# Six broadcast loads per graph, issued by ScalarE instead of SyncE

## The chip, the cores and the metric

The kernel runs on one core of a Trainium2 chip. The metric is the time of one execution on the device in microseconds (us), and a kernel's time is the median of its runs. Engines are called by the names of the profile: PE is TensorE (matrix products; PEld is its weight load), DVE is VectorE, ACT is ScalarE, POOL is GpSimd and SP is SyncE. SPq stands for the instructions that SP's sequencer runs, among them those that issue DMAs.

## The reference, cut to what matters

There are 64 graphs of 256 nodes with 512 features each (x is 64 x 256 x 512), an adjacency matrix of 0 and 1 (64 x 256 x 256), and four layers of the form x = x + layer(relu(layernorm(x))). Layers 0 and 3 weight the rows of a product by a softmax over the nodes, layer 2 is an attention with tanh, and layer 1, in which the change lies, is an attention of 8 heads with one score per node and head for the node itself and one for it as a neighbour:

```python
feats = einsum('bnf,hfu->bhnu', X, W)
e_self = einsum('bhnu,hu->bhn', feats, a_self)
e_neigh = einsum('bhnu,hu->bhn', feats, a_neigh)
dense = leaky_relu(e_self[..., :, None] + e_neigh[..., None, :], 0.2)
dense = dense + NEG_BIG * (1.0 - A[:, None])
out = einsum('bhij,bhju->bhiu', softmax(dense, axis=-1), feats) + b
x = x + relu(out)            # after the heads are put side by side
```

## The kernel before, in words

**Tiles.** All is in float32. A graph's 256 nodes lie on 128 partitions, two to a partition (NC = 2), so that x of one graph is a tile of 128 x 1024 ("xt"). Twenty-three such tiles are the "big" buffers, thirteen of 128 x 512 are the "mid" ones, and eight PSUM tiles the "bank" ones. A step takes a buffer by `Graph.take` (L739) and the last user gives it back with `done` (L748); the next taker in the plan gets it, so a tile's first writer waits for the last reader of what lay there before.

**Order.** Each graph is cut into 209 named steps (`graph`, L1020). No scheduler decides their order: every step has a planned time, written out by hand. `TIMES` (L41) holds them for most graphs; `FIRST` (L85) has own tables for the first nine and `LAST` (L398) for the last eight; graph b's times are moved by b x 52.8 (`PERIOD`, L40). `Plan.sequence` (L703) sorts all steps of all graphs by time, and `Plan.run` (L711) calls them in that order and ties each instruction to the one before it on the same engine. So each of PE, ACT, DVE, POOL and SP runs its instructions in exactly the order of the plan, and the planned times themselves have no other effect. A graph's steps spread over more than 300 us of the plan, so steps of several graphs lie between each other on each engine. Where a step's instruction must wait, all that the plan has after it on that engine waits too. SP issues all DMAs of the kernel before.

**The attention of layer 1.** Its scores lie with the nodes on the partitions (tile `ec`, steps `ec0`, `ec1`), and are needed twice as rows as well, the same row on all 128 partitions. That goes by way of DRAM:

- `send` (L1378): DVE transposes `ec` into `er`.
- `er` (L1382): SP writes `er` to DRAM as `er_d`, in four DMAs (L1386).
- `en0`, `en1` and `es0`, `es1` (`spread`, L1388, with its DMA at L1393): four loads, each of four heads' rows of `er_d`, repeated over 128 partitions: a big tile of 512 KB. The n tiles hold the scores that belong to L1407, the s tiles those that belong to L1445. `en0` and `es1` stand close behind `er` in the plan, `en1` and `es0` later.
- `max0` to `max3` (`largest`, L1399): DVE finds the largest masked score of each row from an n tile and the mask in PSUM (L1407). `mxv`, `mxt` (L1418 to L1430) put it into rows, and `mr` (L1430) has SP write it to DRAM as `m_d`, in four DMAs (L1434).
- `mb0`, `mb1` (`spread` again, L1393): two loads of `m_d`, broadcast in the same way.
- `ea` (L1445, ACT, reads an s tile), `eg` (L1452, POOL, adds the mask), `eb` (L1458, DVE, subtracts the maxima in an m tile), `ex` (L1464, ACT, exp), then `po` (L1476, PE) and `eh` (L1487, POOL), for each of four pairs of heads.

So six loads per graph, 384 in all, go through L1393.

**What lies around them in the plan, of other graphs.** Norms: the squares of a row on ACT (`sx`, L1082), then `rs` (L1088, ACT), the power -0.5 (L1092, POOL), the shift (L1097 and L1098, POOL), and the normed rows (`hn`, L1103, ACT). DVE transposes these (`sq`, L1012), SP writes them to DRAM as `sq_d` (L1123) and gathers them in another order (L1017, L1286; four DMAs each). Sums: `yp` (L1675, ACT) makes one half of a layer's output, and `ya` (L1063, DVE) adds it to x and takes the row sums. ACT also has `om` (L1536, the attention's rows divided by their sums), `am` (L1688, the adjacency by the mask), the copy `va` (L1210), the exponentials of a softmax over nodes (`softa`, L1141 and L1143), its scale (L1152), `aw3` (L1716) and the tanh of layer 2 (`ta`, L1664). DVE's L1202 and L1333 are sums of products; L1657 multiplies by the mask. PE's products are L1188 and L1476 among others.

Of the kernel before, what the change touches and what calls it, by code (L numbers as in the profile page):

```python
# [726 lines left out]
class Graph:  # L727
# [5 lines left out]
    def step(self, name):  # L733
        def add(run):
            self.steps[name] = run
            return run
        return add
# [21 lines left out]
def tile_four_gnn_layers(ctx: ExitStack, tc: tile.TileContext, x, adj, nodemask,  # L759
# [6 lines left out]
    nc = tc.nc  # L766
# [253 lines left out]
    def graph(b):  # L1020

        g = Graph(plan)
# [365 lines left out]
        def spread(name, kind, src, users):  # L1388
            for q in range(2):
                def halves(q=q):  # L1390
                    @step(f"{name}{q}")
                    def _():
                        nc.sync.dma_start(g.take("all", users, name=f"{kind}{q}"),  # L1393
                                          src()[q * HA:(q + 1) * HA].partition_broadcast(P))
                halves()
        spread("en", "n", lambda: st["er_d"][H:], 2)
# [365 lines left out]
```

## Time and profile before

| what | value |
|---|---|
| runs of the kernel before | 3695.48, 3696.07 and 3696.09 us, median 3696.07 |
| the profiled execution's own time | 3695.02 us |
| its span | 3693.2 us |
| PE clock that was granted, mean | 0.981 of full speed |
| instructions | 61,427 |
| DMA: one queue | 70.3% of 16 engines' span, 781 MB |
| idle ahead of DVE's L1012, mostly for ACT's L1103 | 143.6 us |
| idle ahead of DVE's L1407, for er_d loads | 4.1 us |
| idle ahead of DVE's L1458, for m_d loads | 6.5 us |
| idle ahead of ACT's L1445, for er_d loads | 3.1 us |

The profile is of one execution. Its span runs from the first to the last instruction seen, and the 1.8 us by which the execution's own time is longer lie around it. Busy times are sums over an engine's instructions and do not count register, semaphore and DMA-issuing instructions. In a line of a timeline the columns are the start (us from the start of the span), the length (us), the engine, the line of the kernel, the operation, what it writes and reads by the program's names with partitions x elements and type, and how many like it follow each other; an idle time before it stands behind, in brackets, with the instruction that ended it. A line of the waits gives the waiting instruction, the one that it waited for, and the total idle time, how often, and the longest. Who ended a wait is inferred from semaphore events.

### The profile page before, as it was taken

Reading aid. Unit: us, or ns where it says so; the run is one execution under the profiler, and the core shown is the slowest. Engines: PE = TensorE matmul, PEld = TensorE weight load, DVE = VectorE, ACT = ScalarE, POOL = GpSimd, SP = SyncE. Lnnn points to the kernel's source line nnn. Section 1 sums busy time; section 2 is a strip of 40 time slices with the busy share of each in tenths; the row PEclk is TensorE's granted clock in tenths of the full one; section 3 lists DMA queues with packets and bytes.
Section 4 is the critical chain, followed back from the end, with each engine's and each line's share of the span. In section 5 each row is a group of like instructions: output and inputs, shape, how many; then the busy total and the mean of one; then the engine's idle time right before and its main releaser. Section 6 shows DMA issues by size and latency. Waiting matters only on the chain.

```text
span 3693.2 us, 61427 instructions
## 1 busy us (share of the span) xinstructions
PE 3401.5 (92%) x16834; PEld 2175.5 (59%) x16834; DVE 3314.2 (90%) x8248; ACT 2781.7 (75%) x6533; POOL 2270.6 (61%) x2452
## 2 busy tenths in 40 slices
PE   5688999999999999999999999999999999989988
PEld 3455655665665666666666666666666666556554
DVE  6789998999999999999999989999989999999985
ACT  3667777787787787787778778778878778778765
POOL 3565665666666666666666666666666666565653
PEclk8799999999999999999999999999999999999999
DMA  6666766777777777777777777777777777767663
GB/s 185 181 188 208 207 213 212 222 220 216 222 219 218 222 222 217 225 224 224 227 215 221 226 216 217 230 222 219 226 216 219 223 219 221 217 204 216 197 190 119
DMA packets 995143, 785.28 MB, mean 213 GB/s; under 512 B 791984, under 2 KB 862192, under 8 KB 994800
## 3 DMA queue, kind: packets, MB, share of 16 engines
q1 hardware_dynamic: 994800, 781.35, 70.3%
q8 instruction: 137, 2.24, 0.2%
q14 instruction: 206, 1.69, 0.1%
HBM read 511.12 MB, written 270.01 MB: 212 GB/s over the span
## 4 chain that ended last, share of the span: by engine, by line
POOL 22%; DVE 18%; issue 15%; PE 14%; DMA 12%; ACT 7%; SPq 6%; POOLq 0%; ACTq 0%; DVEq 0%
PE bank L1188 9%; DMA big<-sq_d 8%; SPq L1017 5%; DVE big L1458 4%; DVE junk L1407 3%; POOL big L1452 3%; POOL rstd L1092 3%; POOL mid L1487 3%; POOL big L1173 3%; DMA sq_d<-big 3%; POOL big L1172 2%; POOL big L1179 2%; DVE big L1202 2%; DVE big L1012 2%; ACT big L1082 2%
## 5 line engine op out<-in xcount | busy, mean ns | idle before, releaser
L1188 PE MATMUL bank<-t_s,big 128*128 128x264 f32 (+3 forms) x3072 | 978.0, 452 | 8.3 <-DVE big L1657 6.1
L1188 PE MATMUL bank<-w_s,big 128*128 128x264 f32 (+2 forms) x3072 | 850.9, 410 | 45.9 <-DMA big<-sq_d 36.3
L1188 PEld LDWEIGHTS bank<-t_s,big 128*128 128x128 f32 x3072 | 583.0, 194 | 306.5 <-issue 180.5
L1188 PEld LDWEIGHTS bank<-w_s,big 128*128 128x128 f32 x3072 | 583.8, 196 | 278.5 <-issue 131.8
L1452 POOL TENSOR_TENSOR big<-big,mid 128x1024 f32<-128x1024 f32 x256 | 604.0, 2370 | 98.6 <-ACT big L1445 89.0
L1012 DVE STREAM_TRANSPOSE big<-big 128x512 f32<-128x512 f32 x640 | 483.6, 782 | 143.6 <-ACT big L1103 143.5
L1092 POOL TENSOR_TENSOR rstd<-rstd,power 128x2 f32<-128x2 f32 x256 | 183.9, 718 | 678.8 <-ACT rstd L1088 628.2
L1103 ACT ACTIVATE big<-big,shift,rstd 128x512 f32<-128x512 f32 x512 | 387.7, 805 | 167.3 <-POOL shift L1098 167.0
L1172 POOL TENSOR_TENSOR big<-big 128x256 f32<-128x256 f32 x256 | 226.6, 885 | 412.9 <-DMA big<-sq_d 278.7
L1487 POOL TENSOR_TENSOR mid<-big 128x512 f32<-128x512 f32 x256 | 377.1, 1493 | 138.2 <-ACT big L1464 138.2
L1407 DVE CUSTOM_DVE_ANT_0 junk<-big,bank 128x256 f32<-128x256 f32 x1024 | 428.9, 419 | 35.3 <-DMA big<-er_d 4.1
L1082 ACT ACTIVATE big<-big,sum 128x512 f32<-128x512 f32 x512 | 363.8, 712 | 116.7 <-DVE sum L1333 83.7
L1445 ACT ACTIVATE big<-big,ec 128x256 f32<-128x256 f32 x1024 | 428.8, 496 | 5.4 <-DMA big<-er_d 3.1
L1202 DVE TENSOR_TENSOR big<-bank,big 128x320 f32<-128x320 f32 (+1 forms) x704 | 399.5, 571 | 18.2 <-PE bank L1188 13.7
L1476 PE MATMUL bank<-big,big 128*64 128x256 f32 x2048 | 260.7, 388 | 92.2 <-ACT big L1464 91.9
L1458 DVE TENSOR_TENSOR big<-big,big 128x1024 f32<-128x1024 f32 x256 | 325.2, 1309 | 6.5 <-DMA big<-m_d 6.5
L1633 PE MATMUL bank<-big,big 64*128 64x256 f32 x2048 | 283.8, 398 | 50.5 <-DVE mx L1407 31.4
L1657 DVE TENSOR_TENSOR big<-bank,mid 128x512 f32<-128x512 f32 x512 | 319.9, 677 | 5.3 <-PE bank L1633 5.2
L1664 ACT ACTIVATE big<-big 128x512 f32<-128x512 f32 x512 | 293.1, 619 | 14.3 <-DVE big L1657 12.3
L1464 ACT ACTIVATE big<-big 128x1024 f32<-128x1024 f32 x256 | 267.8, 1052 | 41.4 <-DVE big L1458 33.6
L1633 PEld LDWEIGHTS bank<-big,big 64*128 64x128 f32 x2048 | 219.7, 197 | 131.4 <-ACT big L1621 65.1
L1536 ACT ACTIVATE big<-big,rs 128x64 f32<-128x64 f32 x1024 | 257.4, 334 | 24.5 <-DVE rs L1525 13.2
(132 smaller groups left out, 5877.8 us busy)
## 6 DMA issues: line engine op xcount, KB each, us to landing
sq_d<-big SPq DMA_DIRECT2D x448, 512.0 KB
big<-sq_d SPq DMA_DIRECT2D x1792, 128.0 KB
big<-er_d SPq DMA_DIRECT2D x256, 512.0 KB
big<-m_d SPq DMA_DIRECT2D x128, 512.0 KB
big<-in_x_dram SPq DMA_DIRECT2D x64, 512.0 KB
out_dram<-big SPq DMA_DIRECT2D x64, 512.0 KB
mid<-in_adj_dram SPq DMA_DIRECT2D x64, 256.0 KB
mid<-in_adj_dram SPq DMA_DIRECT2D x256, 64.0 KB
```

The source lines that it names most:

```text
L1012: nc.vector.transpose(sq.rearrange("p (r k i c) -> p c k r i", r=4, k=KC, c=NC)[:, c], t[:, c])
L1082: nc.scalar.activation(g["hn"][:, c, :], g["xt"][:, c, :], AF.Square, scale=-float(D), bias=st["sum"][:, c:c + 1], accum_out=st["ssq"][:, ...
L1103: nc.scalar.activation(g["hn"][:, c, :], g["xt"][:, c, :], AF.Relu, bias=st["shift"][:, c:c + 1], scale=st["rstd"][:, c:c + 1])
L1188: nc.tensor.matmul(p, a()[:, k], w[:, k], start=(k == 0), stop=(k == 1))
L1202: nc.vector.tensor_tensor(out(), g[i][:, :w], old(), OP.add)
L1407: nc.vector.tensor_tensor_reduce(junk, g[f"n{h // HA}"][:, h % HA, :], g["far"][:, c * N:(c + 1) * N], 1.0, -BIG, OP.add, OP.max, g["mx"][ ...
L1445: nc.scalar.activation(e[:, s, j, :], g[f"s{h // HA}"][:, h % HA, :], AF.Prelu, bias=st["ec"][:, j, H + h:H + h + 1], alpha=0.2)
L1452: nc.gpsimd.tensor_tensor(e, e, g["negt"][:, None].to_broadcast([P, 2, NC, N]), OP.add)
L1458: nc.vector.tensor_tensor(e, e, g[f"m{p // 2}"][:, p % 2 * 2:p % 2 * 2 + 2, None, :].to_broadcast([P, 2, NC, N]), OP.subtract)
L1487: nc.gpsimd.tensor_tensor(g.take("half", name=f"h{p}"), e[:, :, 0, :], e[:, :, 1, :], OP.add)
L1633: nc.tensor.matmul(ps[s][:, m, :], chunk(g["xpt"][half, p], m), g["xc"][half, p, :], start=True, stop=True)
L1657: nc.vector.tensor_tensor(th[:, s], g[f"ps{p}{s}"].rearrange("p (m n) -> p m n", m=NC), g["at"], OP.mult)
```

## The change

One line of `spread` has another engine issue the DMA. The step's place in the plan, its tiles, the transfer and its source are the same; `Plan.run` ties it to ACT's instruction before it in the plan instead of to SP's.

```diff
@@ -1390,7 +1390,7 @@
                 def halves(q=q):
                     @step(f"{name}{q}")
                     def _():
-                        nc.sync.dma_start(g.take("all", users, name=f"{kind}{q}"),
+                        nc.scalar.dma_start(g.take("all", users, name=f"{kind}{q}"),
                                           src()[q * HA:(q + 1) * HA].partition_broadcast(P))
                 halves()
```

The writes of `er_d` and `m_d` (L1386, L1434), the gathers and all other DMAs stay with SP.

## The prediction

> **What bounds the kernel now.** I read the page's first section, then the waits by engine over the stretch from 734 to 3044 us, in which 43 graphs (12 to 54) run with one and the same order on ScalarE, then the timelines of one of them (graph 32).
>
> ```profile
> PE 3401.5 (92%) x16834; PEld 2175.5 (59%) x16834; DVE 3314.2 (90%) x8248; ACT 2781.7 (75%) x6533; POOL 2270.6 (61%) x2452
> ```
>
> PE and DVE are both near full, ACT has a quarter free. Which of the two binds is seen from who waits: the waits of DVE in that stretch are few (columns: total us, times, longest).
>
> ```profile
> DVE big L1012 <- ACT big L1103: 101.2, 81, 1.5
> DVE bank L1368 <- PE bank L1188: 17.0, 41, 0.4
> DVE big L1270 <- PE bank L1476: 12.7, 42, 1.9
> DVE junk L1407 <- DMA big<-er_d: 1.5, 3, 0.8
> ```
>
> With three smaller ones they are 138 us of 2310: DVE works or steps between instructions for 94% of it, and waits for the six loads 1.5 us in all. So DVE sets the pace, 2310/42 = 55.0 us a graph, and its longest wait is for ACT, by way of ACT, POOL, ACT (a norm). A new wait of DVE is therefore new time, unless an old wait shrinks by as much.
>
> ACT's waits in the same stretch:
>
> ```profile
> ACT big L1082 <- DVE sum L1333: 54.6, 42, 2.5
> ACT big L1082 <- DVE big L1063: 20.0, 41, 1.2
> ```
>
> These two are the slack that I use below: 54.6/43 = 1.27 us and 20.0/43 = 0.47 us a graph. Now the place where the loads go in. SyncE, then ACT, then DVE of graph 32:
>
> ```profile
> 1834.19 1.88 SPq L1386 DMA_DIRECT2D er_d<-er  x4
> 1836.18 2.54 SPq L1017 DMA_DIRECT2D big<-sq_d  x4
> 1839.22 1.30 SPq L1393 DMA_DIRECT2D big<-er_d  x3
> 1843.78 0.32 SPq L1123 DMA_DIRECT2D sq_d<-big  x1
> ```
>
> ```profile
> 1833.41 2.01 ACT L1536 ACTIVATE big<-big,rs 128x64 f32<-128x64 f32 x8
> 1835.33 0.89 ACT L1688 ACTIVATE mid<-mid,mask_c 128x256 f32<-128x256 f32 x2
> 1836.13 0.71 ACT L1082 ACTIVATE big<-big,sum 128x512 f32<-128x512 f32 x1
> ...
> 1837.66 0.72 ACT L1082 ACTIVATE big<-big,sum 128x512 f32<-128x512 f32 x1 [0.73 <-DVE big L1063]
> ...
> 1839.01 1.15 ACT L1675 ACTIVATE big<-big 128x512 f32<-128x512 f32 x2
> 1840.16 1.52 ACT L1103 ACTIVATE big<-big,shift,rstd 128x512 f32<-128x512 f32 x2
> ```
>
> ```profile
> 1839.48 0.69 DVE L1202 TENSOR_TENSOR big<-bank,big 128x512 f32<-128x512 f32 x1
> 1840.08 0.68 DVE L1063 SCALAR_TENSOR_TENSOR big<-big,big 128x512 f32<-128x512 f32 x1
> ```
>
> The reader is to see that er_d is written at 1834.19, that SyncE reads it at 1839.22 only because four gathers stand between, and that ACT is busy right through that time; DVE's L1063 at 1840.08 adds what the first L1675 has written by 1839.64. L1202 just ahead of it has no idle time after it: DVE does not wait here.
>
> **What the Trainium skill says.** "DMA: Bandwidth & Descriptors", section Issuing engines are not separate DMA queues: all issuers feed the same 16 DMA engines, and a second issuer saves only the first one's issue time. All traffic of the trace is on one queue from SyncE, whose issue of such a load takes 426 ns in the median (319 to 1356). The same page, section Anatomy of one DMA: a DMA's semaphore wait is done by the issuing sequencer ahead of the dispatch. The trace agrees: SyncE stood at L1393 for m_d 11.1 us in 19 waits. "Perfetto Trace Analysis", section DVE / Act Engine Instruction: the sequencer pushes compute instructions into a queue where they wait, and goes on. The trace agrees: a semaphore instruction of L1082 ran at 1834.62, ahead of two L1536 and two L1688 that started at 1834.86 to 1835.73, four instructions in front. So an issue with its waits met can hide under queued work; one whose wait is not met stops the sequencer, and the engine runs dry. Same page, section DMA Instruction — HWDGE: an issue locks the descriptor generator, which two sequencers share. No run here shows that yet; it goes into the upper bound.
>
> **The change part by part.** The instruction order of the changed program has 384 DMA issues less on SyncE and 384 more on ACT; the orders of PE, DVE and POOL are the same. In the 43 graphs the places on ACT are: two loads of er_d after the last L1536 and before L1688; a third between L1688 and L1082; the fourth between L1716 and L1103; both loads of m_d between L1143 and L1664.
>
> (1) SyncE loses six issues, 6 x 0.43 = 2.6 us a graph. Worth 0: after the three loads SyncE stood idle from 1840.52 until DVE released L1123 at 1843.78, and after the other ones likewise.
>
> (2) First two er_d loads. They need er_d in memory. The trace's semaphore events tell when each transfer has landed (16 events each): the four er_d writes of graph 32 landed at 1836.84, 1837.15, 1837.33 and 1837.51. ACT is there at 1835.33, so it stops for 2.18 us. Over the 43 graphs the last landing lies 1.90 us after the start of L1688 (1.20 to 3.04). Then come two issues, on SyncE 0.35 and 0.42 us with 0.06 between, some 0.1 for the semaphore instructions ahead and 0.1 to fill the engine again: 1.1 us (estimate from those rows). L1688 is late by 1.90 + 1.1 = 3.0 us. Behind it queue L1688, L1082, L1088, L1210, L1675 and L1103; DVE waits for L1210, L1675 and L1103, POOL for L1088, PE for L1688.
>
> (3) What hides it: the gap of 0.47 us ahead of the second L1082, leaving 2.53; DVE reaches L1063 0.44 us after L1675's half is done (1840.08 against 1839.64; 0.43 to 0.44 in 42 of the 43 graphs), leaving **2.1 us that DVE waits**. The next meeting, L1012 for L1103, had 1.46 us in hand (in three graphs 0.16) and adds nothing. L1141 then waits for DVE, so both are late alike. 43 x 2.1 = **90 us**. DVE's other waits do not shrink: the norms behind them start at a DVE sum (L1333), so they move along.
>
> (4) Third er_d load: 0.38 + 0.05 us under two L1688 of 0.89: 0. Its PE and POOL waits are met by then. Fourth: its data are long there; 0.4 us under the two L1716 (1.3 us): 0, bound 0 to 0.45. It is issued some 3.5 us later than before and lands 5.5 us after, still ahead of L1445, which reads it at 1853.12 before the change and later after.
>
> (5) The m_d loads: m_d lands 0.83 us before L1664 starts in 38 of the 43 (in four 0.1 to 1.5 us after); with 0.97 us for two issues L1664 comes 0.15 to 0.5 us late, and the 1.27 us wait for the sum L1333 after it takes that up: 0. Without that cover 43 x 0.3 = 13 us.
>
> (6) The other 21 graphs, at start and end, have other orders. By the same comparison of landing with ACT's place, er_d stops ACT in graphs 0, 1, 55, 56, 57 (2.8, 2.5, 2.2, 2.9, 2.4 us), m_d in 2, 56, 61 and 63 (6.3, 7.1, 2.1, 7.5 us): 35.8 us. DVE is less full there, so I take half, 18 us (0 to 36), and 5 us for plain issues.
>
> (7) Two queues share the DMA engines in turn. Gathers issued just behind the m_d loads landed after 4.2 us (1861.33 to 1863.25 in graph 32) against 2.7 to 3.0 elsewhere and can gain 1.5; the m_d loads lose up to that and have 1.2 us in hand before L1458. Who waits for those gathers is POOL and PE, not DVE: 0, bounds -0.8 to +0.5 us a graph (-0.8 is all of DVE's waits for PE, 33.0 us over 43).
>
> Sum: 90 + 18 + 5 = 113. The profiled execution took 3695.02 us (span 3693.2), 1 us under the median of 3696.07, so it can stand for it: 3695 + 113 = **3808 us**, 3.1% slower.
>
> **Rivals.** *Absorbed:* the sequencer's four queued instructions, or a faster er_d landing, cover the stop. For it speaks that ACT is idle a quarter of the time; against it that the queue (some 1.2 us) is drained before 1837.5. Needs L1688 under 0.47 + 0.44 = 0.91 us late; gives 3696. *Faster:* the freed gathers, priced at all of DVE's waits for PE: 0.77 x 64 = 49 us, 3646. It decides only below that same 0.91 us, and DVE's waits for PE are mostly behind matmuls whose data were there. *Worse:* each of ACT's issues also waits for SyncE's four gathers, which hold the generator 0.5 to 0.6 us each from 1836.18 to 1838.72: two times 0.6 more, 3.3 x 43 = 142, edges 45: 3882. That the change doesn't do what it says is ruled out by the order.
>
> **How the numbers follow.** This kernel's runs tell a difference above about 0.2% from none. Forecast 0.74, worse 0.14, absorbed 0.06, faster 0.06. Forecast's own range: a DVE wait of 1.2 to 2.7 us a graph (1.90 + x - 0.91, with x, the issues and what lies around them, 0.2 to 1.7 instead of 1.1) and 0 to 41 us of edges, so 3747 to 3852. With most of the worse case it becomes 3745 to 3880, which leaves out the absorbed and the faster case, 0.12 together, and what lies above. Faster 0.06, same 0.06, slower 0.88.
>
> **What would show it.** After: ACT's L1688 idle before it for some 3 us a graph, ended by er_d; DVE's L1063 with a new wait for ACT's L1675 of 2 us a graph; DVE's busy time unchanged; ACT's L1664 hardly late. Wrong if L1063 doesn't wait, if ACT's issues take another length than SyncE's, or if the m_d loads make L1458 wait.

## The result, and the profile after

The changed kernel (called after, as the kernel before is called before) takes 3876.98 us in the median of 4 runs (3871.23 to 3880.58), the kernel before 3695.78 us (3692.90 to 3696.09): a ratio of 1.0491, interval 1.0473 to 1.0509, 181 us more. The profiled execution of after has a span of 3869.5 us, against 3693.2; its own time, 3871.23 us, is 6 us under the median.

The page of after, first section. Busy times are those of before within 1.1%; what falls is the share of the span.

```profile
PE 3436.4 (89%) x16834; PEld 2183.7 (56%) x16834; DVE 3335.0 (86%) x8248; ACT 2782.3 (72%) x6533; POOL 2280.3 (59%) x2452
```

The waits of DVE while graphs 12 to 54 run (767 to 3182 us of after; total us, times, longest). Two lines are new beside the list of before: L1063 waits for ACT's L1675, 76.2/42 = 1.8 us a graph, and L1325 waits for ACT's L1152, 15.4/42 = 0.4 us. L1012 is as it was.

```profile
DVE big L1012 <- ACT big L1103: 102.5, 82, 1.3
DVE big L1063 <- ACT big L1675: 76.2, 42, 3.6
DVE bank L1368 <- PE bank L1188: 17.4, 42, 0.4
DVE big L1325 <- ACT w L1152: 15.4, 42, 2.0
```

ACT's waits in the same stretch. L1688, which never waited before, now does in all 42 cases; the profile files 26 of them under the er_d writes and 16 under "issue", and both are the same stop. The line of L1664 is the place of the two m_d loads.

```profile
ACT mid L1688 <- DMA er_d<-er: 74.4, 26, 4.3
ACT mid L1688 <- issue: 43.3, 16, 3.9
ACT big L1082 <- DVE sum L1333: 39.3, 42, 0.9
...
ACT big L1664 <- DVE tot L1148: 23.9, 40, 1.0
```

Graph 32 in after: SyncE's queue, then ACT, then DVE (start, length, instruction, idle before).

```profile
1914.65 1.76 SPq L1386 DMA_DIRECT2D er_d<-er  x4
1916.51 2.54 SPq L1017 DMA_DIRECT2D big<-sq_d  x4
```

```profile
1913.75 2.02 ACT L1536 ACTIVATE big<-big,rs 128x64 f32<-128x64 f32 x8
1917.59 0.87 ACTq L1393 DMA_DIRECT2D big<-er_d  x2
1918.50 0.51 ACT L1688 ACTIVATE mid<-mid,mask_c 128x256 f32<-128x256 f32 x1 [2.73 <-issue]
1918.61 0.52 ACTq L1393 DMA_DIRECT2D big<-er_d  x1
...
1921.36 1.15 ACT L1675 ACTIVATE big<-big 128x512 f32<-128x512 f32 x2
```

```profile
1919.39 0.68 DVE L1202 TENSOR_TENSOR big<-bank,big 128x512 f32<-128x512 f32 x1
1922.02 0.72 DVE L1063 SCALAR_TENSOR_TENSOR big<-big,big 128x512 f32<-128x512 f32 x1 [1.95 <-ACT big L1675]
```

L1536 ends at 1915.77. The last er_d write landed at 1917.49 (semaphore events of the trace), the first load is issued 0.10 us later, and L1688 starts at 1918.50, 2.73 us after ACT ran dry. DVE is through with L1202 at 1920.07 and stands still for 1.95 us. The third load, at 1918.61, lies beside L1688 and costs nothing. This is the chain that the prediction drew, in the places that it named.

The other new wait, in the same graph. ACT ends L1143 at 1940.75, issues the two m_d loads at 1942.23, and L1664 and L1152 behind them come late for DVE:

```profile
1942.23 0.81 ACTq L1393 DMA_DIRECT2D big<-m_d  x2
1943.09 1.15 ACT L1664 ACTIVATE big<-big 128x512 f32<-128x512 f32 x2 [2.34 <-DVE big L1657]
1944.14 0.28 ACT L1152 ACTIVATE w<-w,tot 128x2 f32<-128x2 f32 x1
```

```profile
1944.46 0.42 DVE L1325 SCALAR_TENSOR_TENSOR big<-big,w,big 128x192 f32<-128x192 f32 x1 [2.05 <-ACT w L1152]
```

The bracket behind L1664 names DVE's L1657. That is not what it waited for: m_d had landed at 1942.21 and the load went out 0.02 us later. Where a DMA issue stands between two instructions of an engine, the bracket can name whatever else came last. (Graph 32 is one of the long cases; in 35 of the 43 ACT stands idle here for 0.56 to 0.58 us, the two issues alone.)

**Where the 176 us are.** I cut both traces at the L1688 of graphs 12 and 54: the start is longer by 32.6 us (734.7 to 767.3), the middle by 105.5 (2309.3 to 2414.8), the end by 38.1. The middle is 76.2 + 15.4 of the two waits, and 11.4 by which four small instructions of DVE have grown (last section); the other 2.5 are the balance of small differences of both signs.

### The profile page after: what moved, and what is told of

It is laid out like the page before. It is cut to its first block, busy times and chain, and to the rows that moved or that the text cites. A ratio compares the mean times of both kernels' runs of the same rounds, so it can differ in the third digit from the quotient of the medians.

```text
span 3869.5 us, 61063 instructions
## 1 busy us (share of the span) xinstructions
PE 3436.4 (89%) x16834; PEld 2183.7 (56%) x16834; DVE 3335.0 (86%) x8248; ACT 2782.3 (72%) x6533; POOL 2280.3 (59%) x2452
## 4 chain that ended last, share of the span: by engine, by line
POOL 21%; DVE 21%; issue 15%; PE 14%; ACT 12%; DMA 11%; SPq 6%; ACTq 0%; POOLq 0%; DVEq 0%
PE bank L1188 9%; DMA big<-sq_d 6%; DVE junk L1407 5%; DVE big L1458 4%; SPq L1017 4%; ACT big L1103 3%; ACT big L1082 3%; POOL rstd L1092 3%; DVE big L1012 3%; POOL big L1173 3%; POOL big L1172 3%; POOL mid L1487 2%; POOL big L1179 2%; DVE big L1202 2%; POOL big L1452 2%
## 5 line engine op out<-in xcount | busy, mean ns | idle before, releaser
L1188 PE MATMUL bank<-w_s,big 128*128 128x264 f32 (+2 forms) x3072 | 852.1, 411 | 46.6 <-DMA sq_d<-big 19.2
L1452 POOL TENSOR_TENSOR big<-big,mid 128x1024 f32<-128x1024 f32 x256 | 603.6, 2368 | 112.9 <-ACT big L1445 105.5
L1012 DVE STREAM_TRANSPOSE big<-big 128x512 f32<-128x512 f32 x640 | 483.3, 781 | 145.7 <-ACT big L1103 145.5
L1103 ACT ACTIVATE big<-big,shift,rstd 128x512 f32<-128x512 f32 x512 | 387.7, 805 | 178.4 <-POOL shift L1098 176.9
L1407 DVE CUSTOM_DVE_ANT_0 junk<-big,bank 128x256 f32<-128x256 f32 x1024 | 428.8, 419 | 52.4 <-DMA big<-er_d 20.5
L1172 POOL TENSOR_TENSOR big<-big 128x256 f32<-128x256 f32 x256 | 226.2, 883 | 404.9 <-DMA big<-sq_d 256.8
L1445 ACT ACTIVATE big<-big,ec 128x256 f32<-128x256 f32 x1024 | 428.8, 496 | 31.0 <-DMA big<-er_d 22.4
L1202 DVE TENSOR_TENSOR big<-bank,big 128x320 f32<-128x320 f32 (+1 forms) x704 | 398.6, 569 | 20.3 <-PE bank L1188 14.5
L1657 DVE TENSOR_TENSOR big<-bank,mid 128x512 f32<-128x512 f32 x512 | 320.4, 677 | 19.4 <-PE bank L1633 15.0
L1458 DVE TENSOR_TENSOR big<-big,big 128x1024 f32<-128x1024 f32 x256 | 326.9, 1315 | 10.8 <-DMA big<-m_d 6.3
L1664 ACT ACTIVATE big<-big 128x512 f32<-128x512 f32 x512 | 290.6, 616 | 51.5 <-DVE tot L1148 25.0
L1063 DVE SCALAR_TENSOR_TENSOR big<-big,big 128x512 f32<-128x512 f32 x256 | 205.9, 819 | 97.2 <-ACT big L1675 89.1
```

Of the source, the lines that this page charges most:

```text
L1012: nc.vector.transpose(sq.rearrange("p (r k i c) -> p c k r i", r=4, k=KC, c=NC)[:, c], t[:, c])
L1103: nc.scalar.activation(g["hn"][:, c, :], g["xt"][:, c, :], AF.Relu, bias=st["shift"][:, c:c + 1], scale=st["rstd"][:, c:c + 1])
L1172: nc.gpsimd.tensor_tensor(m[:, 0], rows_of(1, 0), rows_of(1, 1), OP.add)
L1188: nc.tensor.matmul(p, a()[:, k], w[:, k], start=(k == 0), stop=(k == 1))
L1202: nc.vector.tensor_tensor(out(), g[i][:, :w], old(), OP.add)
L1407: nc.vector.tensor_tensor_reduce(junk, g[f"n{h // HA}"][:, h % HA, :], g["far"][:, c * N:(c + 1) * N], 1.0, -BIG, OP.add, OP.max, g["mx"][ ...
```

## The experiments

The theory after the result: ACT's sequencer takes its instructions in order, so a load placed there stops all later work of ACT until its data are in DRAM, and is itself late where ACT's work ahead of it is late; the cost is that of the place. The rivals: two queues cost as such (issue time, the descriptor generator, transfers that get in each other's way), or the ends of the program pay only for the late middle.

The edits of 1 to 5, 10 and 11 have the same form: a condition that chooses the queue in `spread`. This table cuts each trace as above (us over the kernel before, from one profiled execution each; "all" is the difference of spans):

| kernel | start | middle | end | all |
|---|---|---|---|---|
| after | 32.6 | 105.5 | 38.1 | 176.3 |
| 1 six loads, graphs 12 to 54 | 2.4 | 107.4 | 2.8 | 112.6 |
| 2 six loads, the other graphs | 25.5 | -2.8 | 38.7 | 61.4 |
| 3 en0, es1 | 16.0 | 85.5 | 23.8 | 125.3 |
| 4 mb0, mb1 | 7.7 | 16.8 | 13.5 | 38.0 |
| 5 en1, es0 | 4.9 | 29.7 | 12.0 | 46.6 |
| 6 six loads, er_d replaced by old rows | 31.5 | 41.7 | 45.0 | 118.2 |
| 7 ACT delayed by seven instructions, no load moved | 4.9 | 89.2 | 3.4 | 97.5 |
| 8 ACT delayed by two | 3.5 | 1.3 | 0.9 | 5.7 |
| 9 six loads at later places, graphs 12 to 54 | -1.3 | 15.6 | 3.1 | 17.4 |
| 10 en0, en1, the other graphs | 12.8 | -0.5 | 23.8 | 36.1 |
| 11 es0, es1, the other graphs | 7.3 | -1.3 | 10.7 | 16.7 |
| 12 as 9, m_d loads later still | -0.1 | 0.6 | 2.9 | 3.4 |

**1 and 2, the middle and the ends apart.**

```diff
-                        nc.sync.dma_start(...)
+                        queue = nc.scalar if 12 <= b <= 54 else nc.sync
+                        queue.dma_start(...)
```

```diff
+                        queue = nc.scalar if b < 12 or b > 54 else nc.sync
```

> The six loads on ACT in graphs 12 to 54 only; the other 21 graphs as before. Theory (ACT stops for er_d, DVE is late at L1063, and ACT's stop for m_d makes DVE late at L1325): the 106 us that the trace after shows over these graphs, so 3696 + 106 = 3802 us. Rival (the loss is one of the whole program, two queues hurting each other's transfers): a share of 43/64 of 181, 3818 us, with landing times of the gathers longer everywhere.

> The six loads on ACT in graphs 0 to 11 and 55 to 63 only. Theory: the start and the end cost 29 and 41 us on their own, so 3696 + 70 = 3766 us. As the prediction had it: 3696 + 18 + 5 = 3719 us. Rival (the late middle pushes into the end, so that the end costs less without it): between the two, about 3740 us.

Measured: 3807.82 us, ratio 1.0295 (1.0279 to 1.0310), and 3759.27 us, ratio 1.0168 (1.0151 to 1.0186), both against 3697.30. The first is nearer to the theory's 3802 than to the 3818 of a loss spread over the whole program. 110.5 + 62.0 = 172.5 of 181: the two parts add up within 9 us, and the middle of the second is not slower. The ends have a cost of their own, nearly three times the 23 us of the prediction.

**3, 4 and 5, which loads.**

```diff
+                        queue = nc.scalar if (name, q) in (("en", 0), ("es", 1)) else nc.sync
```

```diff
+                        queue = nc.scalar if name == "mb" else nc.sync
```

```diff
+                        queue = nc.scalar if (name, q) in (("en", 1), ("es", 0)) else nc.sync
```

> Only the first two er_d loads of every graph (en0, es1) on ACT, the other four on SyncE. Theory: L1063 waits as after, 1.8 us a graph with what starts behind it, 82 us in the middle and some half of the 70 us of the ends: 3696 + 82 + 30 = 3808 us; no wait of L1325 for L1152 in the middle. Rival (the loss comes from all six issues, 6 x 0.4 us of ACT a graph): a third of it, 3756 us.

> Only the two m_d loads of every graph (mb0, mb1) on ACT. Theory: L1325 waits for L1152 by 0.3 us a graph as after, 14 us in the middle, and the m_d stops of the ends (graphs 2, 56, 61, 63) 20 us: 3696 + 34 = 3730 us. As the prediction had it: 0 in the middle and some 11 us at the ends, 3707 us.

> Only the third and fourth er_d load of every graph (en1, es0) on ACT. Theory: their data are in memory when ACT gets there, and issues hide under the work that is queued: 0 in the middle; at the ends loads that are issued behind ACT's own work come late, 0 to 15 us: 3696 to 3711 us. Rival (each issue costs ACT its 0.4 us): 64 x 0.8 = 51 us, 3747 us.

Measured: 3822.42 us (1.0339, 1.0324 to 1.0355) and 3736.14 us (1.0111, 1.0094 to 1.0128) against 3697.30; 3743.26 us (1.0115, 1.0100 to 1.0130) against 3698.90. DVE's waits of 3, then of 4 (735 to 3140 us); in 3 the line of L1325 is gone, in 4 that of L1063:

```profile
DVE big L1063 <- ACT big L1676: 72.1, 42, 4.0
```

```profile
DVE big L1325 <- ACT w L1152: 15.2, 43, 1.7
```

(The edit moves later lines by one: L1676 is L1675.) So the er_d loads make the one wait and the m_d loads the other. The three parts sum to 208 us, more than the whole. 5 missed my expectation by 30 us and came near the rival's 3747, but not because each issue costs ACT its time; ACT of graph 32 in 5 tells why:

```profile
1857.13 0.89 ACT L1689 ACTIVATE mid<-mid,mask_c 128x256 f32<-128x256 f32 x2
1859.22 0.33 ACTq L1394 DMA_DIRECT2D big<-er_d  x1
1859.65 0.72 ACT L1082 ACTIVATE big<-big,sum 128x512 f32<-128x512 f32 x1 [1.62 <-POOL big L1179]
```

With the first two loads back on SyncE, the third is the first on ACT to need er_d. That landed at 1859.12, so ACT stops there, two L1688 later than in after (1.52 us in the mean of the 43 graphs), and DVE waits 23.4 us at L1063 in the middle. In after this load is free only because the first had already waited; the parts share one wait and cannot be summed. The bracket again names something else.

**6, the wait taken away.** The loads read rows that were written once at the start.

```diff
+    old = ctx.enter_context(tc.tile_pool(name="old_d", bufs=1, space=DRAM)).tile([E, N], F32, name="old_d")
...
+                if name == "b1":
+                    nc.sync.dma_start(old, t[:E, :N])
...
-        spread("en", "n", lambda: st["er_d"][H:], 2)
+        spread("en", "n", lambda: old[H:], 2)
-        spread("es", "s", lambda: st["er_d"][:H], 2)
+        spread("es", "s", lambda: old[:H], 2)
```

> As after, but the four er_d loads of every graph take their rows from a block in DRAM that is written once at the start (the attention of layer 1 so gets constant scores); er_d is still written. All issues are there, the wait for er_d is not. Theory (the wait is what counts): L1688 at most 0.9 us late, no wait of L1063 in the middle; what stays is L1325's 14 us and the stops for m_d at the ends, so 3696 + 35 = 3731 us. Rival (the issues count): L1688 1.0 us late or more for two issues under a drained queue and the wait of L1063 about 1 us a graph, 3731 + 43 = 3774 us or more.

Measured: 3812.67 us against 3698.90, ratio 1.0299 (1.0282 to 1.0316): far from 3731, and within the rival's "3774 us or more". But the rival's way is not what happened. In the middle L1688 never waits, all three issues lie under L1536 (graph 23, L1539 here), and the eight L1536 ahead of L1688 take 1.93 us, before 1.92:

```profile
1379.01 0.35 ACTq L1396 DMA_DIRECT2D big<-old_d  x1
1379.11 0.58 ACT L1539 ACTIVATE big<-big,rs 128x64 f32<-128x64 f32 x2
1379.46 0.39 ACTq L1396 DMA_DIRECT2D big<-old_d  x1
1379.60 1.05 ACT L1539 ACTIVATE big<-big,rs 128x64 f32<-128x64 f32 x4
1380.39 0.33 ACTq L1396 DMA_DIRECT2D big<-old_d  x1
```

That settles that an issue with its data there costs ACT nothing while work is queued. But the kernel changed more than I meant. DVE still waits 14.0 us at L1063 (L1066 here), in nine graphs; the longest case is this one:

```profile
1389.41 0.69 DVE L1066 SCALAR_TENSOR_TENSOR big<-big,big 128x512 f32<-128x512 f32 x1 [3.94 <-ACT big L1678]
```

L1675 (L1678 here) needed four gathers of L1286, which SyncE had issued from 1377.45 to 1380.03. The last landed at 1388.64, 8.6 us after its issue, and L1675 started 0.11 us later. In the nine cases the last gather took 5.8 to 8.6 us; before the change no gather of L1286 in the middle took more than 4.5. The three loads, which no longer wait for er_d, are in flight beside the gathers: from 1379 to 1385 us the packets of ACT's queue take 63% of the time of the 16 DMA engines and those of SyncE's 22%, where SyncE's had taken 75% in the 2 us before. So a load from one queue can hold up the other queue's transfers, if it starts beside them. The er_d writes come late as well: 4.7 us from issue to landing in the median of the middle, against 2.2 before the change. Part of them are also issued late: the program gives the DMAs of all queues eight completion semaphores in turn (the counters that tell of a landing; 455 or 456 DMAs each before the change), and a DMA waits for the landing of the one eight before it. The third er_d write of graph 23 was issued at 1384.12, 0.01 us after the landing of a load from ACT. So this run is good for L1688 and not for the total. Its ends cost 76.5 us, after has 70.7; but as the slow transfers are in them too, this run doesn't tell what the stop for er_d costs there.

**7 and 8, the delay without the loads.**

```diff
         @step("am")
         def _():
+            for _ in range(7 if 9 <= b <= 51 else 0):
+                nc.scalar.activation(idle_s, idle_s, AF.Copy)
```

(`idle_s` is a tile of 128x256 of its own; in 8 the 7 is a 2. The `am` of graph b stands at the er_d loads of graph b + 3.)

> The kernel before, with seven added ACT instructions of 128x256 (some 0.41 us each, 2.9 us) ahead of L1688 in the middle graphs, and no load moved. Theory (a late ACT at this place is all there is to the er_d part; 0.91 us of it are free): L1063 waits 2.0 us a graph, 43 x 2.0 = 86 us, 3782 us. Rival (two queues matter): no more than ACT's busy time asks, under 40 us.

> The same with two added instructions, 0.82 us. Theory: under the 0.91 us that are free, so within 0.2% of 3696 us and no wait at L1063. Rival (every delay of ACT here is DVE's): 43 x 0.82 = 35 us, 3731 us.

Measured: 3790.61 us, ratio 1.0240 (1.0225 to 1.0255), and 3706.33 us, ratio 1.0020 (1.0011 to 1.0028), against 3698.90. DVE's waits of 7 (L1065 and L1677 are L1063 and L1675):

```profile
DVE big L1014 <- ACT big L1105: 105.6, 84, 1.3
DVE big L1065 <- ACT big L1677: 82.2, 42, 2.6
```

In 7 the added work makes L1688 3.0 us late, and DVE waits 82.2/42 = 2.0 us; in 8 it is 0.76 us late, and L1063 waits 0.8 us over the whole middle, though 8 as a whole is 0.1 to 0.3% slower, at the edge of what can be told. So some 1.0 us is free, near the 0.91 us that the prediction read from two gaps, and a late ACT alone makes the er_d part of the change, without any DMA.

**9 and 12, other places.** The buffers are taken where they were; the issue is a step of its own, with a later time.

```diff
+    "en0_now": 22.500, "es1_now": 22.510, "en1_now": 22.520, "es0_now": 29.000, "mb1_now": 39.360, "mb0_now": 39.370,
...
-                        nc.sync.dma_start(g.take("all", users, name=f"{kind}{q}"),
-                                          src()[q * HA:(q + 1) * HA].partition_broadcast(P))
+                        st[f"{name}{q}"] = g.take("all", users, name=f"{kind}{q}")
+                        if not 12 <= b <= 54:
+                            load(nc.sync)
+
+                    @step(f"{name}{q}_now")
+                    def _():
+                        if 12 <= b <= 54:
+                            load(nc.scalar)
```

In 12 only the last two times differ, 39.500 and 39.510.

> All six loads on ACT in graphs 12 to 54, with buffers taken at the same place, but issued later in ACT's order: the first three er_d loads behind the two L1675 instead of ahead of L1688, the m_d loads behind the first two L1664 and ahead of L1152; the other 21 graphs on SyncE. Theory (it is the place, not the engine): er_d has landed by then, L1063 doesn't wait, L1152 is 0 to 0.3 us late: within 0.3% of the kernel before, 3690 to 3707 us. Rival (two queues cost as such, or ACT pays each issue): 43 x 6 x 0.4 = 103 us at most, 3740 to 3800 us.

> As with the later places, and the m_d loads one step later still: behind L1152, so that DVE's L1325 no longer stands behind them, ahead of the next two L1664. Theory: no wait of L1325 for L1152 (8.6 us less) and none at L1063; the m_d tiles come some 1 us later, which L1458 has in hand: 3715 - 9 = 3706 us, the remainder over the kernel before being DVE's small L1420 to L1427. Rival (loads on ACT cost what they cost wherever they stand): no gain over the later places, 3715 us.

Measured: 9 takes 3714.73 us against 3695.37 (1.0055, 1.0038 to 1.0071), a little more than I had expected. In the middle 9.6 us of it are L1325 waiting for L1152, ahead of which the m_d loads still stand, and 5.8 are the four small instructions of DVE. 12 takes 3695.46 us against 3695.54, ratio 1.0002 (0.9991 to 1.0013), 10 us better than expected: the small instructions too are back within 2.5 us of before. ACT of 12 in graph 32, at the er_d loads (L1685 is L1675), and the head of DVE's waits in its middle, which is the list of before again (L1013 is L1012, L1104 is L1103, and so on):

```profile
1839.51 0.33 ACTq L1404 DMA_DIRECT2D big<-er_d  x1
1839.58 0.63 ACT L1685 ACTIVATE big<-big 128x512 f32<-128x512 f32 x1
1839.86 0.54 ACTq L1404 DMA_DIRECT2D big<-er_d  x1
1840.12 0.62 ACT L1685 ACTIVATE big<-big 128x512 f32<-128x512 f32 x1
1840.44 0.44 ACTq L1404 DMA_DIRECT2D big<-er_d  x1
1840.93 1.52 ACT L1104 ACTIVATE big<-big,shift,rstd 128x512 f32<-128x512 f32 x2 [0.20 <-POOL shift L1099]
```

```profile
DVE big L1013 <- ACT big L1104: 106.4, 87, 1.5
DVE bank L1369 <- PE bank L1189: 17.8, 43, 0.4
DVE big L1271 <- PE bank L1486: 10.9, 43, 1.5
```

258 loads on ACT, at no cost that can be measured, and at no gain: within 0.13%, SyncE's issue time was worth nothing, as step (1) of the prediction had it. No version here beats the kernel before.

**10 and 11, the ends.**

```diff
+                        queue = nc.scalar if name == "en" and not 12 <= b <= 54 else nc.sync
```

```diff
+                        queue = nc.scalar if name == "es" and not 12 <= b <= 54 else nc.sync
```

> Only the loads of the n tiles (en0, en1), and only in graphs 0 to 11 and 55 to 63, on ACT. Theory (at the ends it is mostly the loads that stand behind ACT's work and come late for L1407): L1407 loses 15 to 20 us as after, with ACT's stops for er_d in graphs 0, 1, 2, 10, 11 and 54 to 57 some 30 us, 3728 us. Rival (at the ends too ACT's stops for er_d and m_d are all there is): no loss at L1407, 10 to 15 us, 3710 us.

> Only the loads of the s tiles (es0, es1), and only in graphs 0 to 11 and 55 to 63, on ACT. Theory: no loss at L1407, since the n tiles come from SyncE; L1445 on ACT waits for late s tiles by up to 20 us, of which DVE pays a part: 5 to 20 us, 3703 to 3718 us. Rival: as much as with the n tiles, some 30 us.

Measured, against 3695.37: 3734.39 us (1.0103, 1.0085 to 1.0120) and 3715.36 us (1.0056, 1.0036 to 1.0075). L1407 waited 4.1 us for er_d loads before the change, over the whole run; in after, then in 10 (where L1408 is L1407), it waits:

```profile
DVE junk L1407 <- DMA big<-er_d: 20.5, 10, 4.2
```

```profile
DVE junk L1408 <- DMA big<-er_d: 28.3, 9, 6.5
```

What happens there is seen in after, graph 3. ACT, then DVE:

```profile
235.23 0.30 ACT L1088 ACTIVATE rstd<-ssq,eps 128x2 f32<-128x2 f32 x1
235.37 0.33 ACTq L1393 DMA_DIRECT2D big<-er_d  x1
236.89 0.81 ACT L1103 ACTIVATE big<-big,shift,rstd 128x512 f32<-128x512 f32 x1 [1.37 <-POOL shift L1098]
236.91 0.33 ACTq L1393 DMA_DIRECT2D big<-er_d  x1
```

```profile
239.01 0.42 DVE L1407 CUSTOM_DVE_ANT_0 junk<-big,bank 128x256 f32<-128x256 f32 x1 [3.06 <-DMA big<-er_d]
```

er_d had landed at 230.86; the first load left 4.5 us later, because ACT's own work stood ahead of it, and DVE waited 3.06 us. In nine of the ten waits in after, the load that came late had left 2.9 to 10.4 us after er_d had landed, and ACT was at work for two thirds or more of that time. Over the 21 graphs of the ends the first load leaves 1.77 us after the landing in the mean, at most 6.51 (before 0.88, at most 1.85); in the 43 of the middle it is 0.10, where SyncE took 1.58. The s tiles are late too: ACT's L1445 waits 22.4 us for er_d loads in after, 3.1 before. The n tiles account for 36.6 us of the ends, the s tiles for 18.0, and the m_d loads (start and end of 4) for 21.2, together 75.8; after has 70.7. Of DVE's waits over the ends of after, which grew by 65.7 us, only 17.8 stand at L1407 for these loads; 10.2 are L1063 for L1675, 14.5 are waits for PE, and the rest is spread out. A rival that no run separates: the granted PE clock of the ends was lower after the change (0.92 against 0.93 at the start, 0.95 against 0.98 at the end; 1.00 in the middle of both). It may be a cause of the waits for PE, or their consequence.

## Why the prediction was right and where not

The direction was right, and for the 43 middle graphs the mechanism and the place too, (5) apart. 3876.98 lies outside the forecast's own 3747 to 3852. It lies in the wider range, 3 us under the upper end, by luck: that room was there for slower issues, which did not come, and what filled it came from the ends. The size fell short by 69 us (3808 against 3877). The forecast was 113 us more, and the two profiled executions differ by 176.3; by terms, (3) took 14 us less, (5) 15 more, (6) 48 more, and DVE's small instructions, which had no term, 11 more in the middle.

- **(1)** Right for the middle: 12 shows the moved issues worth 0.
- **(2)** Right within 0.2 us in each number: er_d lands 1.79 us after L1536's end (said: 1.90 after the start of L1688), the two issues and what lies around them take 1.02 us after the landing (said: 1.1), ACT stops for 2.80 us (said: 3.0). "DMA: Bandwidth & Descriptors" of the Trainium skill, section Anatomy of one DMA, which follows a DMA issued by GpSimd, has any semaphore wait done by the issuing sequencer ahead of the dispatch. The trace shows the same of ACT: the load leaves 0.10 us after the landing, and L1688 stands behind it.
- **(3)** Nearly: 1.8 us of DVE's wait instead of 2.1, 76 us for 90. L1012 added nothing, as said.
- **(4)** Right in after; 5 shows that it holds only behind the first two loads.
- **(5)** Wrong. "L1664 comes 0.15 to 0.5 us late" was near (ACT now stands idle 0.66 us ahead of it in the mean), but the cover was looked for at the wrong place, the sum L1333. Between them ACT has L1152, and in the trace before DVE's L1325 started just 0.32 us after L1152 ended. So about 0.66 - 0.32 = 0.34 us a graph pass through; 15.4/42 = 0.37 were measured, where the step had 0. It named 13 us as the price without that cover.
- **(6)** Wrong, and the largest term: 23 us for start and end; 70.7 measured, 62.0 for these graphs alone. The stops themselves came nearly as listed: ACT's time from the end of its work to the issue of a load that had to wait adds up to 39.5 us at the ends of after, where the step had 35.8. What failed is that the step halved them because "DVE is less full there", a guess without a number, and that it counted only where ACT would wait for data and not where data would wait for ACT. L1407's waits for er_d loads grew by 17.8 us at the ends of after, and by 25.7 in 10.
- **(7)** Right for DVE in after: er_d loads landed after 5.46 us in the median against 5.44, m_d loads after 4.99 against 5.36; the gathers of L1017 took 3.19 against 2.98, and no wait of DVE is for them. It isn't so for every place: in 6 the loads start beside SyncE's gathers, and DVE pays 14.0 us.
- **The signs.** L1688 and L1063 waited as said, and L1458 waits 6.3 us for m_d loads where it had waited 6.5. An issue of an er_d load took ACT 0.33 us in the median and SyncE 0.43; another length was named as a sign of being wrong, but 0.1 us moves little. DVE's busy time was said to stay and grew by 20.8 us (3314.2 to 3335.0), 12.9 of it in the four instructions of the last section: a term put at nothing.

Of the rivals, *worse* gave 3882, close to the result, but by another way: it asked for the two issues to take some 2.3 us after the landing, where 1.02 was measured. ACT's loads of graph 32 were issued in the midst of SyncE's gathers (1916.51 to 1919.05), and over the middle an issue that overlaps one of SyncE's took 0.45 us in the median, the others 0.33: some 0.1 us each, not 0.6. That the number is near is chance. *Absorbed* had nearly the right threshold, as 7 and 8 show; the stop was three times that. For *faster* nothing speaks: in 12 the loads cost nothing, and nothing is gained.

What stays open is how the cost of the ends divides between late loads, stops for m_d and for er_d, which overlap, and the lower PE clock; and whether the shared completion semaphores or transfers that meet add to it.

## What to carry to other kernels

A DMA issue that is moved to a compute engine is a wait in that engine's order: price it by where the data are when the engine gets there, and by who waits for what is queued behind, down to the smallest instruction (here a scale of 128x2). Then turn the question round, for every place: how late does the transfer become if the engine is late? And a load that may start sooner can meet transfers that are needed at once (6). With all of these nil, the queue is free to choose (12). The gain was nil too, since the old queue's issue time was not on the path here.

## What the runs showed of the hardware that was not expected

DVE's four instructions on 128x16 (L1418 to L1422) have two lengths. Before, DVE and POOL of one graph:

```profile
1908.03 1.67 DVE L1418 TENSOR_TENSOR mx<-mx,ec 128x16 f32<-128x16 f32 x1
1909.73 0.76 DVE L1420 TENSOR_SCALAR mx<-mx 128x16 f32<-128x16 f32 x1
1910.53 0.17 DVE L1421 SCALAR_TENSOR_TENSOR mx<-mx 128x16 f32<-128x16 f32 x1
```

```profile
1907.31 2.36 POOL L1452 TENSOR_TENSOR big<-big,mid 128x1024 f32<-128x1024 f32 x1
1909.63 0.83 POOL L1172 TENSOR_TENSOR big<-big 128x256 f32<-128x256 f32 x1
```

L1418 ends at 1909.70, 0.03 us after L1452; L1420 at 1910.49, 0.03 after L1172; L1421, which starts 0.01 us ahead of the next POOL instruction, takes 0.17. Over all 256 such instructions before, the 132 that started with POOL at work (for at least 0.15 us more) had a median of 0.79 us and ended 0.03 us after POOL's, the other 124 took 0.175 in the median. "SBUF — State Buffer" of the Trainium skill, section Who interferes with whom, states that a DVE instruction with two inputs in SBUF contends for shared ports with a GpSimd instruction that reads SBUF, and that the first to come holds them for its whole length. The trace agrees for L1418, L1421 and L1422, which have two such inputs. L1420 has one; the page lets its kind contend only in a faster mode that uses two ports, and no run here shows whether it ran in that mode. In after 156 of the 256 met POOL, and their sum grew from 139.6 to 152.5 us: a delay on one engine shifts DVE against POOL, and so changes the length of instructions that the edit never touched. In the waits it can't be seen, since it counts as busy. It isn't always paid: in 8 the four grew by 8.5 us in the middle, and the middle as a whole by 1.3.
